# Attention on one core: projection units reordered, the 128-column score blocks put last, weights turned in score banks, the last half's sums taken on TensorE

## Chip, cores, metric

One core of a Trainium2 chip (trn2), float32 throughout. The metric is the device time of one execution in microseconds (us). Executions of one kernel agree within 0.2%. The experiments were made in four sessions on four chips, each time with the kernel before beside them (medians 1990.3 to 1991.0), so a few tenths of a microsecond between sessions mean nothing. What is read from a trace comes from one profiled execution of each kernel. Engines: PE is TensorE, PEld its weight loads, ACT ScalarE, DVE VectorE, POOL GpSimd, SP the engine that issues most DMAs. A line number such as L255 is a line of the kernel that the profile belongs to, so the numbers shift between kernels.

## What is computed

Batch 32, 256 channels, 1024 positions, 8 heads of 32. Cut to what matters:

```python
def reference(x, q_w, q_b, kv_w, kv_b):
    xn = group_norm(x, groups=32)                      # no scale, no shift
    q = einsum('oc,bcs->bos', q_w, xn) + q_b           # per head: 32 x 1024
    k, v = split(einsum('oc,bcs->bos', kv_w, xn) + kv_b)
    s = q.T @ k / sqrt(32)                             # strictly lower triangle, else -10000
    a = softmax(where(mask == 0, -10000, s)); a = where(mask == 0, 0, a)
    return x + (a @ v.T).T
```

## The kernel before

The score work of one batch is cut into 12 visits. I number them 0 to 11. A visit makes scores for four heads against one key block of 512 columns ("full") and one of 256 ("half"), runs three exponentials on ACT (heads 0 and 1, heads 2 and 3, the half), one projection unit on PE with its eviction on ACT, and then the products with V of the visit before. Scores have six PSUM banks. Projections and key sums (the sums of the exponentials over the keys) share **one** bank (`misc`). In the profile lines sT are scores, pp and ppv projection units (of q or k, and of V), acc the products with V, pd the key sums and den their copy. In visits 1, 5, 7 and 11 the full block of each head is two pieces, of 384 and of 128 columns.

```python
def projections(b):
    qk = [[q unit, k unit] for g in range(2) for hf in range(2)]   # (shortened)
    v = [lambda n=n: project_v(b, n) for n in range(4)]
    return qk[0] + v[:1] + qk[1] + v[1:3] + qk[2] + v[3:] + qk[3]
...
def piece(g, hf, k, part=None):
    d = k - hf * BPH
    if d == 1:                                        # two blocks: 384 and 128 columns
        blocks = [(k, slice(P, HALF), slice(P, HALF)), (k + 2, slice(0, P), slice(3 * P, HALF))]
    ...
def scores(b, full, half):
    ...
    first = [scores_of((b, half), short[:, j % 2, 1, :], j, name) for j in (2, 3)]
    for j in range(4):
        scores_of((b, full), pairs[j // 2][:, j % 2, :], j, name)     # all blocks of a head
    for ins in first:
        ins.then_inc(bank_free, 1)
    wait = nc.tensor.wait_ge(bank_free, live["free"])                 # "the gate"
    for j in range(2):
        lo = scores_of((b, half), short[:, j, 0, :], j, name)         # late products
    for a in range(2):
        nc.scalar.activation(e[:, 2 * a : 2 * a + 2, :], pairs[a], AF.Exp)
    exp = nc.scalar.activation(eh..., short, AF.Exp)
    mask(full, e); mask(half, eh)                                     # on GpSimd
...
for i in range(B * N + 1):                 # the order on every engine is the program's
    scores(i // N, *visits[i % N])
    for f in at.pop(i, ()): f()            # a projection unit with its eviction
    values((i - 1) // N, ...)              # products with V, DVE adds exponentials up
    for f in after.pop(i, ()): f()         # key sums (pd), norm statistics (pm, pv), finishes
...
# last batch: rows of sums of three halves fetched at N-2, inverted and broadcast at N-1
```

## Time and profile before

| | before |
|---|---|
| median of 3 runs | 1991.79 us (1989.82 to 1992.19) |
| span of the profiled run | 1990.4 us |
| first scores / start of the second batch (visit 12) | 22.77 / 88.68 us |
| one steady batch, score start to score start | 60.61 us |
| last batch's start / last score group's start / end | 1907.12 / 1958.62 / 1990.4 us |

I read the kernel as three parts: a start up to the second batch, thirty equal batches, and the last batch with the end. A hundredth of a microsecond in one visit of every batch is 0.3 us of the time. The visit lengths below are means over the steady batches, from the starts of the first score product of each visit. The profile lines of before stand in the prediction.

### The profile page before, as it was taken

To read this page: it belongs to the slowest core of one execution; us is meant where nothing else is said; L and a number is where in the kernel's file an instruction comes from. 1 tells how busy PE (TensorE), PEld (TensorE's weight loads), DVE (VectorE), ACT (ScalarE), POOL (GpSimd) and SP (SyncE) were. 2 spreads that over 40 slices of the span, in tenths; PEclk is the share of its full clock that TensorE was granted. 3 is DMA by queue.
4 is the path that set the end of the run, shared out by engine and by line. 5 is a ranking of instruction groups with operands and counts; after the bars stand their busy time and mean duration, and the time that the engine had idled before them with its cause. 6 is when DMAs were issued, how large, how long until landed. Compare 5 with 4: busy or idle time off the path is not lost.

```text
span 1990.4 us, 54612 instructions
## 1 busy us (share of the span) xinstructions
PE 1941.6 (98%) x24078; PEld 961.9 (48%) x24078; DVE 1559.4 (78%) x1608; ACT 1462.8 (73%) x1863; POOL 580.1 (29%) x495
## 2 busy tenths in 40 slices
PE   6999999999999999999999999999999999999995
PEld 3444544444544445545444454454444454544442
DVE  3787878877878877878878788778788787887777
ACT  4777777777777777777777777777777777777773
POOL 1323323323223323233233233232232332332321
PEclk9999999999999999999999999999999999999997
DMA  2011111111111111111111111111111111111011
GB/s 104 2 67 41 51 47 65 66 51 47 54 52 66 67 41 51 52 61 66 59 43 52 49 66 67 41 51 55 57 66 67 35 54 49 66 66 45 31 35 68
DMA packets 56800, 108.04 MB, mean 54 GB/s; under 512 B 14189, under 2 KB 15341, under 8 KB 56557
## 3 DMA queue, kind: packets, MB, share of 16 engines
q1 hardware_dynamic: 54780, 103.56, 14.7%
q8 instruction: 191, 3.13, 0.7%
q10 hardware_dynamic: 1776, 0.92, 0.2%
q14 instruction: 53, 0.43, 0.1%
HBM read 68.82 MB, written 35.64 MB: 52 GB/s over the span
## 4 chain that ended last, share of the span: by engine, by line
PE 91%; ACT 5%; issue 2%; DVE 1%; DMA 1%; ACTq 0%; POOL 0%; SPq 0%; DVEq 0%
PE sT L255 29%; PE pp L147 24%; PE acc L325 23%; PE ppv L147 9%; PE pd L343 6%; ACT e L302 3%; ACT v L225 1%; ACT eh L303 1%; DMA rb<-inverses 0%; DVE e L330 0%; DMA qk_bias<-in_L_conv_q_b_dram 0%; PE pm L147 0%; PE pv L147 0%; DVE rb L389 0%; DVE rb L388 0%
## 5 line engine op out<-in xcount | busy, mean ns | idle before, releaser
L302 ACT ACTIVATE e<-sT 128x1024 f32<-128x1024 f32 x768 | 744.9, 1022 | 278.5 <-PE sT L255 232.4
L330 DVE TENSOR_TENSOR e<-e,eh 128x1024 f32<-128x1024 f32 x384 | 543.8, 1430 | 384.0 <-PE acc L325 363.4
L270 POOL TENSOR_SCALAR_AFFINE_SELECT e<-e 128x512 f32<-128x512 f32 (+1 forms) x256 | 390.7, 1526 | 1360.9 <-ACT e L302 1185.4
L330 DVE TENSOR_TENSOR e<-e,e 128x1536 f32<-128x1536 f32 (+2 forms) x384 | 638.2, 1662 | 17.3 <-POOL e L270 2.0
L255 PE MATMUL sT<-q,k 32*128 32x256 f32 (+3 forms) x7168 | 618.1, 460 | 0.8 <-ACT k L209 0.8
L255 PEld LDWEIGHTS sT<-q,k 32*128 32x128 f32 x7168 | 463.3, 184 | 203.6 <-issue 106.7
L147 PE MATMUL pp<-xn,wT 128*32 128x512 f32 x4096 | 495.9, 602 | 2.4 <-DVE xn L192 0.9
L325 PE MATMUL acc<-e,v 128*32 128x512 f32 (+2 forms) x4096 | 400.7, 486 | 0.9 <-POOL e L270 0.9
L303 ACT ACTIVATE eh<-sT 128x1024 f32<-128x1024 f32 x384 | 396.0, 1031 | 0.0
L147 PE MATMUL ppv<-wT,xn 128*32 128x256 f32 x4096 | 247.6, 382 | 1.3 <-ACT k L209 1.3
L325 PEld LDWEIGHTS acc<-e,v 128*32 128x32 f32 x4096 | 132.6, 110 | 224.9 <-issue 200.4
L325 PE MATMUL acc<-eh,v 128*32 128x256 f32 x3072 | 225.1, 380 | 9.5 <-ACT v L225 9.5
L147 PEld LDWEIGHTS pp<-xn,wT 128*32 128x32 f32 x4096 | 107.3, 109 | 230.2 <-issue 216.6
L348 ACT COPY den<-pd 128x512 f32<-128x512 f32 x128 | 75.0, 586 | 187.7 <-PE pd L343 187.7
L325 PEld LDWEIGHTS acc<-eh,v 128*32 128x32 f32 x3072 | 96.2, 110 | 182.6 <-issue 134.0
L147 PEld LDWEIGHTS ppv<-wT,xn 128*32 128x32 f32 x4096 | 120.0, 109 | 96.8 <-issue 20.6
L270 POOL TENSOR_SCALAR_AFFINE_SELECT eh<-eh 128x512 f32<-128x512 f32 x128 | 164.1, 1282 | 2.6
L343 PE MATMUL pd<-e,pick 128*32 128x512 f32 x1024 | 135.7, 599 | 7.1 <-DVE e L330 7.1
L389 DVE SCALAR_TENSOR_TENSOR rb<-rb,v_bias_col,x 128x512 f32<-128x512 f32 x129 | 96.5, 748 | 4.6
L209 ACT ACTIVATE q<-pp,qk_bias 128x512 f32<-128x512 f32 x128 | 89.8, 702 | 6.3 <-PE pp L147 6.3
L209 ACT ACTIVATE k<-pp,qk_bias 128x512 f32<-128x512 f32 x128 | 89.8, 702 | 3.8 <-PE pp L147 3.8
L388 DVE TENSOR_TENSOR rb<-num,rb 128x512 f32<-128x512 f32 x129 | 87.7, 680 | 1.6 <-DMA rb<-inverses 1.5
(45 smaller groups left out, 497.7 us busy)
## 6 DMA issues: line engine op xcount, KB each, us to landing
x<-in_x_dram SPq DMA_DIRECT2D x64, 512.0 KB
rb<-inverses SPq DMA_DIRECT2D x127, 256.0 KB
out_dram<-rb SPq DMA_DIRECT2D x127, 256.0 KB
sums<-den SPq DMA_DIRECT2D x128, 8.0 KB
rows<-sums SPq DMA_DIRECT2D x31, 32.0 KB
inverses<-inv SPq DMA_DIRECT2D x31, 32.0 KB
wn<-in_L_conv_kv_w_dram ACTq DMA_DIRECT2D x2, 256.0 KB
wn<-in_L_conv_q_w_dram ACTq DMA_DIRECT2D x1, 256.0 KB
```

Source lines behind the costliest of these rows:

```text
L147: nc.tensor.matmul(out[part], lhsT=lhsT[:, part], rhs=rhs, start=start, stop=stop, skip_group_check=True)
L209: nc.scalar.activation(live[key][:, cols], pp, AF.Identity, bias=qk_bias[:, n, g : g + 1], scale=(SCALE, 1.0)[n],)
L255: ins = nc.tensor.matmul(pair[:, cols], lhsT=live["k", b, g][rows, kb * P : (kb + 1) * P], rhs=live["q", b, g][rows, hf * HALF + of.start ...
L270: nc.gpsimd.affine_select(out=diagonal, in_=diagonal, pattern=[[0, 4], [0, n], [1, P]], compare_op=ALU.is_gt, fill=0.0, base=0, channel_mu ...
L302: nc.scalar.activation(e[:, 2 * a : 2 * a + 2, :], pairs[a], AF.Exp)
L303: exp = nc.scalar.activation(eh.rearrange("p (n bank) q -> p bank n q", n=2), short, AF.Exp)
L325: nc.tensor.matmul(acc[HD * j : HD * (j + 1), of], lhsT=live["v", b][:, kb, h * HD : (h + 1) * HD], rhs=e[:, j, cols], start=first, stop=l ...
L330: nc.vector.tensor_add(total[:, :, of], total[:, :, of], e[:, :, cols])
L343: nc.tensor.matmul(pd[HD * j : HD * (j + 1), :], lhsT=pick, rhs=total[:, j, :], start=True, stop=True, skip_group_check=True,)
L348: nc.scalar.copy(den, pd)
L388: nc.vector.tensor_mul(rb[:, g, cols], num[:, g, cols], rb[:, g, cols])
L389: nc.vector.scalar_tensor_tensor(rb[:, g, cols], rb[:, g, cols], v_bias_col[:, g : g + 1], xt[:, g, cols], ALU.add, ALU.add)
```

## The change

Its intent, part by part: take away a wait for V in visit 1 by making V earlier; put the 128-column blocks after everything else so that they fill the score group better; start the weights in idle score banks and keep PE's clock up with filler products; take the last half's sums on PE instead of adding on DVE, and split the last batch's inversion so that part of it runs early.

```diff
-            return qk[0] + v[:1] + qk[1] + v[1:3] + qk[2] + v[3:] + qk[3]
+            return qk[0] + v[:2] + qk[1] + v[2:] + qk[2] + qk[3]
@@ scores
             for j in range(4):
-                scores_of((b, full), pairs[j // 2][:, j % 2, :], j, name)
+                scores_of((b, full), pairs[j // 2][:, j % 2, :], j, 0)      # 384 (or all) columns
             (gate and late products as before)
-            for a in range(2):
-                nc.scalar.activation(e[:, 2 * a : 2 * a + 2, :], pairs[a], AF.Exp)
-            exp = nc.scalar.activation(eh..., short, AF.Exp)
+            two = len(full[4]) == 2
+            if two:
+                for j in range(4):
+                    scores_of((b, full), pairs[j // 2][:, j % 2, :], j, 1)  # 128 columns
+            for a in (2, 0, 1) if two else (0, 1, 2):                       # 2 is the half bank
+                (the same exponentials)
@@ start: weights turned in score banks, fillers, first projections in two banks
+            load_weights(); turn_weights(0); norm_channels...; keep_busy(4)
+            norm_mean(0); turn_weights(1); norm_deviation(0); norm_variance(0); norm_rstd(0)
+            turn_weights(2); keep_busy(6)
@@ last batch
+                        for i in (N - 1, N):      # the last pieces summed on PE, into one bank
+                            when(first + i, lambda b=b, i=i: sum_pieces(b, products[i - 1], i == N - 1, i == N), after)
-                    when(first + N - 2, lambda b=b: gather(b, every[:3]))
-                    (check and invert three halves at N - 1)
+                    for v, ns in ((N - 4, every[:2]), (N - 2, every[2:3])):
+                        when(first + v, lambda b=b, ns=ns: gather(b, ns))
+                        when(first + v + 1, lambda b=b, ns=ns: check_sums(b, ns))
+                        when(first + v + 1, lambda b=b, ns=ns: invert(b, ns))
```

Not in the cut: the first projections take turns in two banks, the scaling of the biases goes from GpSimd to DVE, and the final check and count of the sums go ahead of the last two finishes. The rest of the diff moves code and gives helpers a name.

## The prediction

> **What bounds the kernel now.** I read the page first, then the waits of the steady part, then the timeline of single visits, then both ends.
>
> ```profile
> PE 1941.6 (98%) x24078; PEld 961.9 (48%) x24078; DVE 1559.4 (78%) x1608; ACT 1462.8 (73%) x1863; POOL 580.1 (29%) x495
> ...
> PE 91%; ACT 5%; issue 2%; DVE 1%; DMA 1%; ACTq 0%; POOL 0%; SPq 0%; DVEq 0%
> ```
>
> TensorE (PE) holds the path nearly everywhere. A batch is 12 visits; I number them 0 to 11. On PE a visit is: scores (sT), one projection unit (pp or ppv), the value products of the visit before (acc), sometimes key sums (pd). Score starts in the trace put a batch at 60.6 us in the whole steady part, each visit the same to within some ns. So a change per visit is paid 31 or 32 times. In the steady part the table of waits holds two lines that matter:
>
> ```profile
> PEld pd L343 <- ACT k L209: 10.5, 29, 0.4
> ...
> PE acc L325 <- ACT v L225: 8.6, 29, 0.3
> ```
>
> The second is one wait per batch, in visit 1, for a V eviction. The timeline of PE in visit 1, and of PE and ScalarE (ACT) in visit 7, which has the same work without that wait:
>
> ```profile
> 1002.73 1.67 PE L255 MATMUL sT<-q,k 32*128 32x256 f32 x24
> 1004.33 1.93 PE L147 MATMUL ppv<-wT,xn 128*32 128x256 f32 x32
> 1006.08 1.04 PE L325 MATMUL acc<-e,v 128*32 128x512 f32 x8
> 1007.42 0.64 PE L325 MATMUL acc<-eh,v 128*32 128x256 f32 x8 [0.30 <-ACT v L225]
> 1007.85 1.07 PE L343 MATMUL pd<-e,pick 128*32 128x512 f32 x8
> ```
>
> ```profile
> 1033.46 1.67 PE L255 MATMUL sT<-q,k 32*128 32x256 f32 x24
> 1035.06 1.92 PE L147 MATMUL pp<-xn,wT 128*32 128x512 f32 x16
> 1036.80 1.04 PE L325 MATMUL acc<-e,v 128*32 128x512 f32 x8
> 1037.66 0.61 PE L325 MATMUL acc<-eh,v 128*32 128x256 f32 x8
> 1038.15 1.06 PE L343 MATMUL pd<-e,pick 128*32 128x512 f32 x8
> ```
>
> ```profile
> 1034.67 1.94 ACT L302 ACTIVATE e<-sT 128x1024 f32<-128x1024 f32 x2 [0.52 <-PE sT L255]
> 1036.50 1.03 ACT L303 ACTIVATE eh<-sT 128x1024 f32<-128x1024 f32 x1
> 1037.40 0.70 ACT L209 ACTIVATE k<-pp,qk_bias 128x512 f32<-128x512 f32 x1
> ```
>
> Read start to start: from the acc start to the pd start is 1.77 us in visit 1 and 1.35 in visit 7, so the V wait costs 0.42 us a batch. But see visit 7: the k eviction ends at 1038.10 and pd starts at 1038.15. There is one bank for projections and sums, ACT does the three exponentials before the eviction, and pd waits for it. PE has **no slack left** against ACT there: what delays the exponentials delays pd.
>
> At the two ends:
>
> ```profile
> 13.82 3.64 PE L147 MATMUL pp<-xn,wT 128*32 128x512 f32 x16 [0.86 <-DVE xn L192]
> 18.32 3.64 PE L147 MATMUL pp<-xn,wT 128*32 128x512 f32 x16 [0.86 <-ACT q L209]
> 22.77 1.57 PE L255 MATMUL sT<-q,k 32*128 32x256 f32 x16 [0.81 <-ACT k L209]
> ```
>
> ```profile
> 1971.90 1.93 PE L343 MATMUL pd<-e,pick 128*32 128x512 f32 x8 [7.07 <-DVE e L330]
> ```
>
> The first projections take 3.64 us where steady ones are 1.75 apart, and at the end PE waits 7 us for VectorE (DVE) sums.
>
> **What the Trainium skill says.** (1) "TensorE: Matmul & The Clock Gate", Part 1, "What's actually happening": the clock is halved until PE has been busy for a window of about 3.4 us. Agrees: the 3.64 us above are twice the later ones, and the granted clock first reads full at 22.0 us, after unbroken work from 18.3. (2) Same page, Part 3, "The mechanism": a weight load is pulled ahead of running products only for another row group. The four heads of a score group are four row groups; the trace shows each row's next load start as its previous product starts, so order within a row matters. (3) "Perfetto Trace Analysis", "Matmuls": independent groups should rotate through PSUM banks, so evictions overlap. The pd wait of visit 7 is what one bank costs. (4) Same page, "Tensor Engine Instruction": ACT and DVE are strict first-in first-out, and ends of products are estimates; so I measure start to start on PE, and take ACT's order as fixed.
>
> **V units moved.** The order of units goes from qk v qk v v qk v qk to qk v v qk v v qk qk, a qk being two units. V1 is now done two visits before its use: the wait of visit 1 goes, 0.42 us. In exchange the rest slides one visit later. q of the second half is now made in visit 0 and used by the first scores of visit 1; k of the second group is made in visit 5 and used by the first scores of visit 6. In visit 0 the eviction ends 4.62 us after the visit's start and PE wants it at 4.65: with a 0.05 lag that costs 0.02. Visit 5 is worked out below, since it also has the second change.
>
> **128-column blocks last.** Four visits (1, 5, 7, 11) have them. Their score group lasts 1.60 us to the next start, against 1.50 in the others (1008.85 to 1010.35): 0.10 is to be won. But the two late 256-column products wait on a semaphore for the first two to end. In an ordinary visit that gate opens 0.79 us in:
>
> ```profile
> 1009.64 0.19 PEld L255 LDWEIGHTS sT<-q,k 32*128 32x128 f32 x2
> ```
>
> A row that holds only 384 columns before the gate is idle from about 0.75; with a fresh load (0.11) it streams again at 0.90. Then 256 columns (0.43) and 128 (0.21) end at 1.54, and the next group starts 0.09 later: 1.63. So I expect **no gain, some 0.03 loss**: the small blocks had filled that gap.
>
> The larger effect is on ACT. In these visits the exponential of the half bank now goes first, and its products lie behind the gate: 0.79, plus 0.70 from a fresh load to the end of two such products (first pair of a group), plus 0.05 for the semaphore: the first exponential starts at 1.54. Before it was 1.21 (1034.67 less 1033.46). The eviction ends 3.43 after that start (1038.10 less 1034.67), pd or a dependent score starts 0.05 later: 1.54 + 3.48 = 5.02 us into the visit.
> - Visit 7: pd at 5.02 instead of 4.69 (1038.15 less 1033.46): +0.33.
> - Visit 1: now a k unit; pd at 5.02 instead of 5.12: -0.10 is all that remains of the 0.42.
> - Visit 5: now a k unit that the next scores need: length 5.02 instead of 4.76: +0.26.
> - Visit 11: a V unit, nobody waits: +0.03. Visit 0: +0.02.
> Sum: +0.54 a batch. Times 31, and about 0.6 for the first batch, which has no pd in visit 1: **+17 us**.
>
> **The start.** Weights are turned in score banks, so no pool stands in the way; the bias scaling leaves GpSimd's queue, where it held the averaging matrix back until 10.3 us; the group statistics can go once the fillers end. Four fillers of 256 columns at half clock are some 0.85 each: 6.1 to 9.5 at most. From that product to the first projection took 3.47 (10.35 to 13.82); the six further fillers (0.43 warm, 0.85 cold) end about 1 us after that. So projections start near 14.2, but warm: 2 x 1.75, then 0.85 for the last eviction, and no wait between them since the second has its own bank. First scores at 18.5 instead of 22.77: -4.3. Visit 0 lasted 10.3 us with three units waiting for one bank; I get 1.50 + 3 x 1.75 + 0.8 for an eviction + 0.2 = 7.75: -2.5. Visit 1 gives 0.5. Together **-7**.
>
> **The end.** The last half's sums leave DVE: its additions ran from 1964.4 to 1971.9. PE instead sums pieces while it waits for masks, and adds 1.3 us after the last values: pd complete near 1967.7, against 1973.8. Then one eviction (0.6), two reciprocals of 1.75, one finish (1.5), the check of the sums, whose two small transfers now lie beside the reciprocals, and 1.8 for the last finish: DVE ends near 1976.5 instead of 1984.7. The three 256 KB transfers that landed at 1976.4 become one. The branch at the end is not shortened (5.7 us). **-8**, with 1 or 2 either way.
>
> Sum: 1991.8 + 17 - 7 - 8 = 1994. Changes of this kind are mostly kept because they paid, so I shade to **1992**.
>
> **Rivals.** (a) The author's sum: the V wait gone (0.42) and 0.10 in four visits, 0.82 x 31 = 25 us, and 15 at the ends: 1952. For it: both terms are visible in the trace. Against it: pd at 1038.15 sits on an eviction at 1038.10, and the exponentials can't start before the gate. (b) The blocks do give the 0.10 because the gate opens earlier than in ordinary visits, and the exponentials start near 1.40: visits 1, 5, 7 then give -0.24, +0.13, +0.19, visit 11 -0.10, so the steady part is even and the time 1977. (c) ACT is late as I say, and DVE or GpSimd masks, which start later too (after the third exponential), come too late for the value products of visits 6 and 0: I get some 0.1 to 0.4 us of room; if it is gone, up to 0.3 more in two visits, 2010.
>
> **Range and chances.** My mechanism about 0.75, (b) or something between it and (a) 0.2, (c) 0.05. The ends are uncertain by 3 us, the steady sum by 4. Range 1978 to 2001. More than 2% faster means under 1952, only (a) in full: 0.03. Slower than 2032: 0.005.
>
> **What would show it.** In the profile after: batches of 61.1 us between score starts (60.6 before; under 60.3 and I am wrong); no wait of acc for v; pd in visits 1 and 7 about 5.0 us after the score start with a k eviction ending just before; the first scores of visit 6 waiting for a k eviction; the first exponential of the four visits 1.5 us in; their score group at 1.60 or more to the next start; first scores near 18.5; the last DVE instruction 8 us nearer to the last values. If pd in visit 7 starts at 4.7, the ACT step is wrong and the time is near 1970.

## The result, and the profile after

The changed kernel took **2000.82 us** (median of 4 runs, 2000.64 to 2001.10) against 1991.81 for the kernel before on the same chip. The ratio is 1.0047, interval [1.0030, 1.0065]: within 2%, but clearly slower. Ratios here are the mean time of one kernel's runs over that of the other's of the same rounds, so not quite the ratio of the medians.

| part, from the two traces | before | after | difference | predicted |
|---|---|---|---|---|
| start to visit 12 | 88.68 | 81.80 | -6.9 | -6.4 |
| 30 steady batches | 30 x 60.61 | 30 x 61.25 | +19.1 | +16.2 |
| last batch and end | 83.28 | 79.65 | -3.6 | -7.5 |
| span | 1990.4 | 1999.0 | +8.6 | +2.3 |

The "predicted" column sorts the prediction's own terms: -7 and the first batch's +0.6; 30 times 0.54; -8 and the last batch's 0.54.

The steady visits, in us:

| visit | 0 | 1 | 4 | 5 | 7 | 11 | batch |
|---|---|---|---|---|---|---|---|
| before | 4.652 | 6.117 | 4.837 | 4.754 | 5.691 | 4.744 | 60.61 |
| after | 4.670 | 6.019 | 4.894 | 5.024 | 6.019 | 4.801 | 61.25 |

First the page of the changed kernel, the two lines that answer to those of before:

```profile
PE 1957.1 (98%) x24138; PEld 957.4 (48%) x24138; DVE 1588.5 (79%) x1607; ACT 1461.6 (73%) x1860; POOL 546.2 (27%) x494
...
PE 64%; ACT 13%; issue 10%; DVE 8%; POOL 2%; DMA 2%; SPq 0%; ACTq 0%; DVEq 0%; POOLq 0%
```

PE is still busy 98%, yet its share of the chain fell from 91% to 64% and ACT's rose from 5% to 13%: busy time hides it, the chain shows it. Then the waits of the steady part (what waited for what: us in total, times, longest):

```profile
PEld pd L358 <- ACT k L221: 37.3, 58, 0.6
...
PEld sT L267 <- ACT k L221: 18.7, 29, 0.6
```

Before, the first of these was 10.5 us and 29 times. The line of V products waiting for a V eviction (8.6 us before) is gone. So the wait that the change aimed at was removed, and another took its place. The timeline of visit 7 shows which, PE first and then ACT:

```profile
1036.42 1.72 PE L267 MATMUL sT<-q,k 32*128 32x256 f32 x24
1038.07 1.92 PE L159 MATMUL pp<-xn,wT 128*32 128x512 f32 x16
...
1041.44 1.06 PE L358 MATMUL pd<-e,pick 128*32 128x512 f32 x8 [0.16 <-ACT k L221]
```

```profile
1037.96 1.02 ACT L320 ACTIVATE eh<-sT 128x1024 f32<-128x1024 f32 x1 [0.85 <-PE sT L267]
1038.88 1.94 ACT L322 ACTIVATE e<-sT 128x1024 f32<-128x1024 f32 x2
1040.69 0.70 ACT L221 ACTIVATE k<-pp,qk_bias 128x512 f32<-128x512 f32 x1
```

ACT's first exponential starts 1.54 us into the visit (1037.96 less 1036.42; before 1.21). The four ACT instructions then run without a gap, the eviction ends at 1041.39, and pd starts at 1041.44, 5.02 into the visit (before 4.69). The score group itself lasts 1.65 (1038.07 less 1036.42; before 1.60). In visit 5 the same eviction holds the next visit's scores:

```profile
1031.58 0.71 PE L267 MATMUL sT<-q,k 32*128 32x256 f32 x4 [0.16 <-ACT k L221]
```

The visit started at 1026.56, so it lasted 5.02. The bracketed 0.16 is only the idle time directly ahead of the product; weight loads and the modelled ends hide the rest, which is why start to start is the measure.

At the start (PE):

```profile
13.76 3.64 PE L159 MATMUL pp<-xn,wT 128*32 128x512 f32 x32
18.21 1.57 PE L267 MATMUL sT<-q,k 32*128 32x256 f32 x16 [0.81 <-ACT k L221]
```

Two units in 3.64 us, where before one took that; first scores at 18.21 instead of 22.77. At the end (DVE):

```profile
1975.24 1.23 DVE L349 TENSOR_TENSOR e<-e,eh 128x1024 f32<-128x1024 f32 x1
1980.60 0.22 DVE L401 SCALAR_TENSOR_TENSOR in_range<-rows,in_range 32x64 f32<-32x64 f32 x1 [4.13 <-DMA rows<-sums]
...
1984.53 3.36 DVE L435 RECIPROCAL rb<-pd 128x256 f32<-128x256 f32 x2
1989.41 0.69 DVE L423 TENSOR_TENSOR rb<-num,rb 128x512 f32<-128x512 f32 x1 [1.52 <-DMA rb<-inverses]
```

DVE stood 4.13 us in front of the check of the third half's sums, and behind that check were the finishes and the last reciprocals. PE had the last half's sums complete at 1981.46, 3.1 us before those reciprocals began. SP's queue tells why the rows came so late:

```profile
1970.77 1.16 SPq L414 DMA_DIRECT2D rb<-inverses  x2
1971.98 0.51 SPq L386 DMA_DIRECT2D sums<-den  x1
...
1979.01 0.34 SPq L396 DMA_DIRECT2D rows<-sums  x1
```

The 8 KB of sums were issued at 1971.98, just behind two broadcasts of 256 KB each, and had landed only by 1979.0, when the fetch could go. The chain that ended last (followed back through the profile of the changed kernel) runs through this transfer (6.96 us), and later through that of the **last** half's sums: 5.13 us from 1985.09, behind the third half's broadcast of 256 KB, issued at 1983.67. DVE waited 0.67 us for the rows of that one, so the two chains end close together.

### The profile page after: what moved, and what is told of

Read it like the earlier page. It is cut to its first block, busy times and chain, and to the rows that moved or that the text cites. A ratio compares the mean times of both kernels' runs of the same rounds, so it can differ in the third digit from the quotient of the medians.

```text
span 1999.0 us, 54756 instructions
## 1 busy us (share of the span) xinstructions
PE 1957.1 (98%) x24138; PEld 957.4 (48%) x24138; DVE 1588.5 (79%) x1607; ACT 1461.6 (73%) x1860; POOL 546.2 (27%) x494
## 4 chain that ended last, share of the span: by engine, by line
PE 64%; ACT 13%; issue 10%; DVE 8%; POOL 2%; DMA 2%; SPq 0%; ACTq 0%; DVEq 0%; POOLq 0%
PE sT L267 22%; PE acc L344 14%; PE pp L159 12%; PE ppv L159 9%; DVE e L349 7%; ACT e L322 7%; PE pd L358 6%; ACT eh L320 4%; ACT k L221 3%; POOL e L282 2%; DMA sums<-den 1%; DMA wn<-in_L_conv_kv_w_dram 0%; PE pm L159 0%; DMA x<-in_x_dram 0%; PE pv L159 0%
## 5 line engine op out<-in xcount | busy, mean ns | idle before, releaser
L349 DVE TENSOR_TENSOR e<-e,eh 128x1024 f32<-128x1024 f32 x382 | 551.8, 1458 | 334.1 <-PE acc L344 313.9
L282 POOL TENSOR_SCALAR_AFFINE_SELECT e<-e 128x512 f32<-128x512 f32 (+1 forms) x256 | 386.4, 1509 | 1414.4 <-ACT e L322 1146.0
L349 DVE TENSOR_TENSOR e<-e,e 128x1536 f32<-128x1536 f32 x381 | 635.2, 1667 | 44.8 <-POOL e L282 33.5
L267 PEld LDWEIGHTS sT<-q,k 32*128 32x128 f32 x7168 | 454.5, 184 | 225.5 <-issue 107.0
L358 PE MATMUL pd<-e,pick 128*32 128x512 f32 (+1 forms) x1048 | 136.7, 595 | 11.6 <-ACT k L221 10.2
L282 POOL TENSOR_SCALAR_AFFINE_SELECT eh<-eh 128x512 f32<-128x512 f32 x128 | 107.4, 839 | 0.1
```

The lines of the kernel that those rows point to most:

```text
L267: ins = nc.tensor.matmul(pair[:, cols], lhsT=live["k", b, g][rows, kb * P : (kb + 1) * P], rhs=live["q", b, g][rows, hf * HALF + of.start ...
L282: nc.gpsimd.affine_select(out=diagonal, in_=diagonal, pattern=[[0, 4], [0, n], [1, P]], compare_op=ALU.is_gt, fill=0.0, base=0, channel_mu ...
L349: nc.vector.tensor_add(total[:, :, of], total[:, :, of], e[:, :, cols])
L358: nc.tensor.matmul(pd[HD * j : HD * (j + 1), of], lhsT=pick, rhs=e[:, j, cols], start=start, stop=stop, skip_group_check=True,)
```

## The experiments

Theory **A**: the steady loss is ACT's. The half bank's exponential goes first and has to wait for the late products; the eviction comes behind three exponentials; pd (visits 1, 7) and the next scores (visit 5) wait for the eviction. Rivals: the score group of PE itself got longer; V's new place costs; the masks come late. Theory **T** for the end: the third half's small transfers, not the last half's sums. "End" in the table is from the start of the last score group to the end of the span; among the thirteen it is 26.6 to 28.3 wherever the tail works as in the changed kernel.

| run | ratio to before | median, us | batch, us | end, us |
|---|---|---|---|---|
| before | 1 | 1991.8 | 60.61 | 31.8 |
| after | 1.0047 | 2000.82 | 61.25 | 27.62 |
| r1_blocks_back | 0.9885 [0.9869, 0.9902] | 1968.06 | 60.21 | 27.22 |
| r2_units_back | 1.0079 [1.0063, 1.0096] | 2006.78 | 61.42 | 27.96 |
| r3_both_back | 0.9947 [0.9931, 0.9964] | 1980.45 | 60.61 | 27.09 |
| r4_before_gate | 0.9970 [0.9953, 0.9987] | 1984.96 | 60.78 | 26.89 |
| r5_evict_early | 0.9895 [0.9879, 0.9912] | 1970.63 | 60.28 | 27.82 |
| r6_by_pairs | 0.9857 [0.9841, 0.9874] | 1962.83 | 60.07 | 26.58 |
| r7_no_fill | 1.0050 [1.0033, 1.0067] | 2001.09 | 61.25 | 27.39 |
| r8_tail_queue | 1.0040 [1.0023, 1.0057] | 1999.49 | 61.26 | 25.77 |
| r9_tail_order | 1.0056 [1.0039, 1.0072] | 2001.21 | 61.26 | 27.27 |
| r10_best_a | 0.9808 [0.9792, 0.9824] | 1952.33 | 59.69 | 28.27 |
| r11_best_b | 0.9786 [0.9769, 0.9802] | 1947.61 | 59.50 | 27.69 |
| r12_tail_direct | 1.0031 [1.0014, 1.0048] | 1997.47 | 61.26 | 24.07 |
| r13_best_c | 0.9765 [0.9749, 0.9781] | 1944.54 | 59.50 | 25.15 |

All were correct.

### 1. Each steady part taken back by itself

Blocks and exponentials as before (r1), with V moved and the new ends:

```diff
-                scores_of((b, full), pairs[j // 2][:, j % 2, :], j, 0)
+                scores_of((b, full), pairs[j // 2][:, j % 2, :], j)
-            if two: (the 128-column blocks after the gate)
-            for a in (2, 0, 1) if two else (0, 1, 2):
+            for a in (0, 1, 2):
```

> The changed kernel with the score order inside a visit as before: each head's 128 columns right after its 384, exponentials of the two pairs first. V units stay moved, both ends stay changed. Theory A (the late exponential delays the eviction that PE waits for): the first exponential is back at 1.21 us into visits 1 and 7, so pd starts at 4.69 in both; visit 1 is 5.69, visit 7 is 5.69, visit 5 is 4.76, visit 11 is 4.75; a batch is 60.25 us between score starts (61.25 in the changed kernel), and the time is about 1969. Rival B (the block order costs only its 0.05 us of PE in four visits, and the moved units cost the rest): a batch is 61.05, visits 5 and 7 stay near 5.0 and 6.0, the time is about 1994.

Units as before from the second batch on (r2), with the blocks last:

```diff
+            if b:
+                return qk[0] + v[:1] + qk[1] + v[1:3] + qk[2] + v[3:] + qk[3]
             return qk[0] + v[:2] + qk[1] + v[2:] + qk[2] + qk[3]
```

> The changed kernel with the V units of batches 1 to 31 where they were; 128-column blocks stay last, ends stay changed. Theory A: visit 1 holds a V unit whose eviction ends near 4.87, so the second value products start at 4.92 and pd at 5.35: visit 1 is 6.35; visit 7 stays 6.02; visit 5 is 4.80, since nothing waits for a V eviction there; a batch is about 61.3 us, the same as the changed kernel, time 2000 to 2003: with blocks last, moving the V units is worth nothing. Rival B (moved units are what costs): a batch near 60.8, time about 1987.

Both of these edits together (r3), which leaves only the new ends:

> Only the two ends changed; the steady part as in the kernel before. Every theory: a batch of 60.61 us, and the start and the end worth what the traces show, 7.5 and about 4 us: 1980. If the time is over 1984, the ends are worth less than I read from the traces.

Measured: r1 1968.06 with visits 1, 5, 7, 11 at 5.691, 4.744, 5.690, 4.754; r2 2006.78 with visit 1 at 6.448 (I had expected 6.35), visit 5 at 4.800, visit 7 at 6.019; r3 1980.45. The expectation of r2 missed: with the blocks last I had thought the moved units worth nothing and the time 2000 to 2003. ACT in visit 7 of r1, which starts at 1019.83 and lasts 5.69:

```profile
1021.04 1.94 ACT L318 ACTIVATE e<-sT 128x1024 f32<-128x1024 f32 x2 [0.52 <-PE sT L267]
1022.86 1.03 ACT L316 ACTIVATE eh<-sT 128x1024 f32<-128x1024 f32 x1
1023.76 0.70 ACT L221 ACTIVATE k<-pp,qk_bias 128x512 f32<-128x512 f32 x1
```

First exponential at 1.21, as in the kernel before. What follows: against r3, moving the units alone gives 0.40 us a batch (60.61 to 60.21), as large as the V wait was. Putting the blocks last alone costs 0.81 (60.61 to 61.42). Together they cost 0.64: with the blocks last the moved units still give 0.17 (61.42 to 61.25), and not 0.40, because they put into visit 5 a k that the next scores need, exactly where the eviction became late (visit 5 is 4.800 in r2, 5.024 in the changed kernel). The ends are worth 10.5 us (r3).

### 2. The eviction put ahead of the third exponential

In visits 1, 5 and 7 only ACT's order changes: half bank, heads 0 and 1, eviction, heads 2 and 3; GpSimd masks the half first.

```diff
-                (exponential of heads 2, 3 and both masks inside scores())
+                late = scores(i // N, *visits[i % N], early=i % N in (1, 5, 7))
                 for f in at.pop(i, ()):      # the unit and its eviction
                     f()
+                for f in late:               # exponential of heads 2, 3, then its mask
+                    f()
```

> The changed kernel, with nothing altered on PE: in visits 1, 5 and 7 alone ScalarE evicts the projection before its third exponential instead of after it (and GpSimd masks the half bank first). Theory A (PE waits for an eviction that stands behind three exponentials): the eviction runs from about 3.6 to 4.3 us, PE waits for nothing there, and pd starts at its own pace, 4.68 us into visits 1 and 7, whose length falls from 6.02 to 5.68; visit 5 falls from 5.02 to 4.79. A batch is 60.35 us, the time about 1972. Rival B (PE's order of products is what costs): nothing moves, 2001. Rival D (ScalarE has no room, so the late third exponential takes back the gain through the score banks or the masks): visits 2, 6 and 8 grow by up to 0.3 each, 1980 to 1990.

Measured: 1970.63; visits 1 and 7 at 5.649, visit 5 at 4.791; PE's program is that of the changed kernel, and its score group still lasts 1.64 (1022.71 less 1021.07). PE and ACT in visit 7, which starts at 1021.07:

```profile
1021.07 1.72 PE L267 MATMUL sT<-q,k 32*128 32x256 f32 x24
1022.71 1.92 PE L159 MATMUL pp<-xn,wT 128*32 128x512 f32 x16
...
1025.75 1.04 PE L366 MATMUL pd<-e,pick 128*32 128x512 f32 x8
```

```profile
1022.61 1.02 ACT L321 ACTIVATE eh<-sT 128x1024 f32<-128x1024 f32 x1 [0.79 <-PE sT L267]
1023.53 1.02 ACT L325 ACTIVATE e<-sT 128x1024 f32<-128x1024 f32 x1
1024.71 0.69 ACT L221 ACTIVATE k<-pp,qk_bias 128x512 f32<-128x512 f32 x1 [0.16 <-PE pp L159]
```

The first exponential is as late as in the changed kernel (1.54), but the eviction ends 4.33 into the visit instead of 4.97, pd starts at 4.68 instead of 5.02, and the visit is 0.37 shorter. So it is not PE's group that costs, and not the late exponential as such: it is **the eviction in line behind it**. This is what shows theory A. Visit 6's score group grew by 0.06, but the visit did not (4.839; 4.836 in the changed kernel), so the late third exponential cost no time that can be seen.

### 3. The blocks ahead of the gate, in two orders

A cheaper way to use ACT's time would be small blocks that don't delay the exponentials. First (r4) all 384-column blocks, then all 128-column blocks, then the gate, exponentials as before:

```diff
             for j in range(4):
                 scores_of((b, full), pairs[j // 2][:, j % 2, :], j, 0)
+            if len(full[4]) == 2:
+                for j in range(4):
+                    scores_of((b, full), pairs[j // 2][:, j % 2, :], j, 1)
             (gate, late products; no blocks after them; exponentials 0, 1, 2)
```

> V units moved, ends changed, the 128-column blocks of all four heads after all 384-column ones but before the gate, exponentials of the two pairs first. Theory A: no row idles at the gate and no load comes late, so the score group of visits 1, 5, 7, 11 takes 1.50 us to the next start (1.60 before, 1.65 changed); the first exponential starts near 1.18, pd at 4.66 in visits 1 and 7 (their length 5.66), visit 5 is 4.74, visit 11 is 4.65: a batch of 60.1, time about 1964. Rival C (128-column products cost extra wherever they stand, since a weight load takes longer than they do): the group stays at 1.60 and a batch at 60.25, as in the run with the blocks put back.

This missed: 1984.96 instead of 1964. The score group became 1.51 as expected, but the first exponential started at 1.42, not 1.18. ACT in visit 7 of r4, which starts at 1028.77:

```profile
1030.19 1.94 ACT L321 ACTIVATE e<-sT 128x1024 f32<-128x1024 f32 x2 [0.73 <-PE sT L267]
```

In the records of single products, the blocks of heads 0 and 1 that this exponential reads had ended 1.15 into the visit. The 384-column blocks of heads 2 and 3, which it doesn't read but which stand ahead of the 128-column blocks in the program, ended at 1.34. (The records don't name the head; I tell them apart by size and order.) So I put up theory **A2**: a wait for PE is met when everything up to the awaited product in program order is done. That the exponential waited for a later product instead is ruled out if the modelled ends are right: the next products of the visit that raise the semaphore which ACT waits for ended at 1.57 and 1.58, after it had started. The next kernel (r6) keeps pairs of heads together, heads 0 and 1 first:

```diff
-            for j in range(4):
-                scores_of((b, full), pairs[j // 2][:, j % 2, :], j, 0)
+            for a in range(2):
+                for n in range(len(full[4])):
+                    for j in (2 * a, 2 * a + 1):
+                        scores_of((b, full), pairs[a][:, j % 2, :], j, n)
```

> V units moved, ends changed; in the four visits the order is heads 0 and 1: 384 columns, then their 128; then heads 2 and 3 likewise; then the gate and the late products; exponentials of the pairs first. In the run with all 384-column products first, the first exponential started at 1.43 though its own products ended at 1.14: it started 0.08 after products of heads 2 and 3 that stand before them in the program (end 1.35). Theory A2 (a wait for PE counts all products up to that place in the program): with the pairs kept together the first exponential starts at 1.20, the group takes 1.51, visits 1 and 7 are 5.68, visit 5 is 4.74, visit 11 is 4.66, a batch 60.1, the time about 1965. Rival (the exponential was late for another reason, a bank written by the other heads): it stays at 1.43 and the time at 1985.

Measured: 1962.83; visits 1 and 7 at 5.673, 5 at 4.729, 11 at 4.667; group 1.51. ACT in visit 7, which starts at 1017.47:

```profile
1018.66 1.94 ACT L320 ACTIVATE e<-sT 128x1024 f32<-128x1024 f32 x2 [0.50 <-PE sT L267]
1020.49 1.03 ACT L318 ACTIVATE eh<-sT 128x1024 f32<-128x1024 f32 x1
1021.39 0.70 ACT L221 ACTIVATE k<-pp,qk_bias 128x512 f32<-128x512 f32 x1
```

The first exponential is at 1.19. What makes the pair a clean test: in the two kernels every one of the 24 score records of visit 7 starts within 0.01 us of the same offset. PE did the same at the same times; only the program order, and with it what the exponential waited for, differs, and the exponential moved by 0.23 us.

### 4. The start without fillers

```diff
-            keep_busy(4)
-            keep_busy(6)
```

> The changed kernel without its ten filler products at the start. If the fillers are worth the whole start gain, the first scores fall back from 18.2 to 22.7 us, and the time to 2005. My reading: without them the group statistics go 1 us earlier and the first projections follow at once, cold (3.64 us each, no wait between them) until a window of work has passed; first scores between 18.0 and 20.0, time 2000.5 to 2002.5.

Measured: 2001.09, first scores at 18.50:

```profile
11.93 5.77 PE L159 MATMUL pp<-xn,wT 128*32 128x512 f32 x32 [1.03 <-DVE xn L204]
18.50 1.57 PE L267 MATMUL sT<-q,k 32*128 32x256 f32 x16 [0.81 <-ACT k L221]
```

Without fillers the first two units take 5.77 us instead of 3.64, but start 1.83 earlier (11.93 against 13.76), since the group averages no longer stand behind fillers. First scores in the other runs lie between 17.9 and 18.8, so the fillers are worth nothing that can be measured. The gain of the start must be in the rest, which no run shows part by part: no pool and no GpSimd work ahead of the averaging matrix, a second bank for the first projections, and a shorter first visit (10.28 to 7.76).

### 5. The end

First (r8) the last batch's broadcasts were issued from GpSimd's queue, out of the way of the small transfers:

```diff
-                nc.sync.dma_start(out=live["rb", b][...], in_=live["inv", b][n]...broadcast_to(...))
+                (nc.gpsimd if b == B - 1 else nc.sync).dma_start(...)
```

> The changed kernel; in the last batch alone the broadcasts of the inverses leave from GpSimd's queue, so the small transfers of the sums do not stand behind them on SyncE's. Theory T (the third half's 8 KB transfer, issued at 1971.98, ended only at 1979.0 because 512 KB of broadcasts were ahead of it on the same queue, and VectorE waited 4.1 us for it in order): it lands in about 2 us, the wait goes, and from the last score start to the end takes about 23.5 us instead of 27.6; the time is about 1997. Rival (the 16 engines are full, whatever the queue): the transfer still takes 5 us or more, the end is within 1 us of 27.6, the time 2000 to 2001.

Measured: end 25.77, a gain of 1.85 where 4 was expected, and 0.8 below the least of the others. DVE's wait went from 4.13 to 2.58:

```profile
1980.24 0.22 DVE L401 SCALAR_TENSOR_TENSOR in_range<-rows,in_range 32x64 f32<-32x64 f32 x1 [2.58 <-DMA rows<-sums]
```

The fetch of the rows was issued at 1973.78 instead of 1979.01, but the rows still took until about 1980.2: they landed 0.2 us after the second of the broadcasts (1980.01). So the queue is a part of it, the company of other transfers another: the 512 KB of broadcasts, and a store of 256 KB that SP had issued at 1973.39, just ahead of the fetch; r8 doesn't tell these two apart. The last half's 8 KB gained more: issued at 1985.06 while the third broadcast was under way on GpSimd's queue (1982.81 to 1988.81), they took 1.70 us instead of 5.13. The edit also had a side effect: GpSimd issued the broadcasts from 1972.21 on and so came late with its masks, and PE's products with V waited for them:

```profile
1976.63 1.94 PE L344 MATMUL acc<-e,v 128*32 128x512 f32 x8 [2.09 <-POOL e L282]
```

The last half's sums were complete 12.1 us after the last score group's start instead of 10.1. The end didn't hang on that, since DVE stood 0.40 us for the third half's broadcast behind the reciprocals. Second (r9), the broadcasts were to be issued after the fetch:

```diff
-            for n in ns: (broadcasts inside invert)
+            if not (b == B - 1 and ns.start == 0):
+                spread(b, ns)
+                    when(first + N - 2, lambda b=b: spread(b, every[:2]))   # after the gather of half 3
```

> The changed kernel, with one edit in the last batch: the two broadcasts of inverses for the first channel group are issued after the sums of the third half have been fetched back, so the two small transfers no longer stand behind 512 KB. Theory T (the end lost what I expected because the small transfers stood behind the broadcasts, and DVE, in order, waited 4.1 us for them): the rows of the third half land near 1976, DVE's wait of 4.1 us for them goes, and last score to end falls from 27.6 to 24 to 25.5 us. Rival (the end is set by the chain through the last sums and two reciprocals, the wait is only slack in it): 27 or more. Steady part unchanged, time 1997 to 1999 under T.

This **tested nothing**. Only PE, ACT, DVE and GpSimd keep the program's order in this kernel; SP's queue is ordered by the scheduler, which put the broadcasts first again:

```profile
1971.24 1.16 SPq L418 DMA_DIRECT2D rb<-inverses  x2
1972.44 0.51 SPq L386 DMA_DIRECT2D sums<-den  x1
```

Third (r12), no transfer at all ahead of the reciprocals: DVE inverts the third half's sums straight from their bank, and its rows are fetched later with the last half's, for the check alone.

```diff
+        def invert_third(b):
+            for c in range(2):
+                within = slice(c * HALFBANK, (c + 1) * HALFBANK)
+                nc.vector.reciprocal(live["rb", b][:, NG - 1, within], live["pd", b, 2][:, within])
-                    for v, ns in ((N - 4, every[:2]), (N - 2, every[2:3])):
+                    for v, ns in ((N - 4, every[:2]),):
+                    when(first + N, lambda b=b: invert_third(b))
-                    for n in every[:2]: (finish)
+                    for n in every[:3]: (finish)
-            check_sums(B - 1, every[3:])
+            check_sums(B - 1, every[2:])
```

(The last half's sums move to a score bank, so that the two don't share one.)

> The changed kernel with one edit in the last batch: VectorE takes the inverses of the third half from its sums in the bank (two reciprocals of 1.7 us) instead of from rows that two small transfers bring and a broadcast brings back; the rows are fetched with the last half's for the check alone, and the last half's sums use a score bank. Theory T (the small transfers stood between the additions and the reciprocals): no wait of 4.1 us for rows; additions end near 1976.5, third half's reciprocals to 1980, finishes to 1984.5, last reciprocals to 1988, check and last finish to 1991: last score to end 23.5 to 24.5 instead of 27.6. Rival (the end hangs on the last half's own sums on PE and the check of them): 26.5 or more. Steady part unchanged; time 1996 to 1998 under T.

Measured: end 24.07, 3.5 less than the changed kernel, as expected. DVE:

```profile
1976.00 1.23 DVE L349 TENSOR_TENSOR e<-e,eh 128x1024 f32<-128x1024 f32 x1
1977.14 3.36 DVE L442 RECIPROCAL rb<-pd 128x256 f32<-128x256 f32 x2
...
1984.91 3.36 DVE L435 RECIPROCAL rb<-pd 128x256 f32<-128x256 f32 x2
1989.06 0.22 DVE L401 SCALAR_TENSOR_TENSOR in_range<-rows,in_range 64x64 f32<-64x64 f32 x1 [0.79 <-DMA rows<-sums]
```

DVE no longer waits between additions and reciprocals; it pays 3.36 us of extra reciprocals and still ends earlier, because the third half's finish no longer waits for a broadcast that comes back at 1989.4. From the last score group's start to DVE's last instruction it takes 19.8 us here, 23.3 in the changed kernel, 26.0 before. Theory T is shown as far as the third half's round trip goes (two small transfers, check, broadcast), which r12 takes off the path as a whole. Its rival, that PE completes the last half's sums too late, falls: they were complete 10.1 us after the last score group's start in the changed kernel and 10.2 in r12. One thing changed along with it: the transfer of the last half's sums took 1.70 us (from 1985.40) instead of 5.13, now that no broadcast stood ahead of it, and what that alone is worth is not shown.

### 6. A faster version

The order by pairs, with early evictions too, the pairs' first exponential leading: in visits 1, 5 and 7 (r10), and in visits 0, 4 and 6 as well (r11).

```diff
+                late = scores(i // N, *visits[i % N], early=i % N in (1, 5, 7))             # r10
+                late = scores(i // N, *visits[i % N], early=i % N in (0, 1, 4, 5, 6, 7))    # r11
+            for a in (0, 2, 1) if early else (0, 1, 2):   # heads 0,1; half; eviction; heads 2,3
```

> Pairs of heads kept together (as in the run by pairs), and in visits 1, 5 and 7 the exponential of heads 0, 1 first, then the half bank, then the projection's eviction, then the exponential of heads 2, 3; last batch as in the run before. Theory A2 (what is left of the loss in visits 1, 5 and 7 is the eviction behind three exponentials): visits 1 and 7 near 5.55, visit 5 near 4.65, batch 59.75, time 1950 to 1954. Rival (with the eviction early, masks or score banks become the bound, as visit 6's score group of 1.56 hinted): batch 59.95 or more, time 1957 or more.

> As the run before, with the early eviction in visits 0 and 4 and 6 too. Theory: visits 0 and 4 were 4.67 and 4.89 in the changed kernel, because their evictions end late; early they lose up to 0.15 each, batch 59.6, time 1946 to 1950. Rival (masks late, score banks freed late): batch no shorter than in the run before.

Measured: r10 1952.33, visits 1 and 7 at 5.515, visit 5 at 4.657, batch 59.69; visit 6's score group is 1.56, as the rival had it, but the visit is no longer for it (4.841; 4.836 in r6). r11 1947.61, batch 59.50: visit 4 went from 4.838 to 4.681 and visit 6 from 4.841 to 4.743, and visits 1, 5 and 7 gave up to 0.05 of it back. Both kernels still carry r9's edit, which does nothing. With r12's end instead (r13):

> The fastest steady part so far (pairs of heads together, early evictions in visits 0, 1, 4, 5, 6, 7: 1947.6 us, batch 59.50) with the end of the run before. If the two add: 1944 to 1946, batch 59.50. If the end is set by something else once visits are shorter: 1947 or more.

Measured: 1944.54, ratio 0.9765: the gains add (1947.61 less 1944.54 is 3.1), and the kernel beats the one before by 2.35%.

## Why the prediction was right or wrong, point by point

**Right: what bounds the kernel and which wait replaces which.** The first exponential was predicted at 1.54 and came at 1.54; pd and the end of visit 5 at 5.02 and came at 5.02; the V wait went; scores of visit 6 wait for k. Visits 0, 1, 5 and 7 came within 0.01 us of the predicted lengths. Experiments 1 and 2 show the cause as the prediction gave it. Rival (a) saw both terms of the gain rightly, since r1 gets the V wait's 0.40 and r6 a part of what the group gives (60.21 to 60.07 a batch), but not that this order of the blocks forfeits them. Rival (b) needed exponentials at 1.40 and a shorter group; neither came. Rival (c), late masks, was not needed for any of it.

**A little off: the size of the steady term, +0.54 against +0.64.** Visit 4 is missing from the sum. It grew by 0.057: its exponentials start at 1.25 instead of 1.19, so its eviction ends later, and the group averages wait for the bank. r11, which lets that eviction go first, takes 0.16 off visit 4, so it too was bound by ACT, which I had not looked at. The packed trace shows where the 0.06 comes from: in the changed kernel ACT has one more semaphore instruction there (an instruction that only waits; the views leave these out), at 1.19, where the exponential otherwise starts, and the exponential follows at 1.25. It is there in every steady visit 4 of the seven kernels whose visit 4 starts its exponentials at 1.25 (the changed one, r2, r5, r7, r8, r9, r12) and in none of the eight that start them at 1.19; PE's score products in that visit are at the same offsets. So it comes with the blocks put last, whether the units are moved or not. Of the rest, 0.03 is in visit 11: the group is 1.65, not 1.63. Over thirty batches this is 2.9 us.

**Right in size, in part by luck: the start**, -6.9 against -6.4: the first scores came 4.6 earlier (4.3 predicted), visit 0 was 2.5 shorter, as predicted. But the part I gave to the warm clock was wrong: I reckoned projections "near 14.2, but warm", and they were, yet without fillers the same scores come at 18.50 instead of 18.21.

**Wrong: the end.** This is the largest miss: of the 6.3 us by which the sum of the terms fell short (2.3 against 8.6), 3.9 are here, 2.9 in the steady part, and the start gave 0.5 back. The prediction said -8; the changed kernel gained 4.2 there from the last score group on (31.8 to 27.6; the 3.6 of the table has the last batch's longer visits in it). The step that failed is the list that follows "pd complete": "one eviction (0.6), two reciprocals of 1.75, one finish (1.5), the check of the sums, whose two small transfers now lie beside the reciprocals". It has no term for the **third** half, whose sums now go out alone, behind the two broadcasts that the same change had moved early; they took 7 us to land, and DVE, which takes its work in order, stood 4.13 us with the reciprocals behind it. Then, with the reciprocals done, it waited 1.52 more for the broadcast that comes of them: so the third half's round trip held the end here, and not the late reciprocals. The last half's sums were mis-sized too: pd was complete 10.1 us after the last score group's start, where the prediction had 9.1 (1967.7 less 1958.62), and their own transfer, not sized at all, took 5.13 us and ended on the path as well. I had counted it a gain that "The three 256 KB transfers that landed at 1976.4 become one". r12 takes these transfers off the path, and the end is 7.7 us shorter than before. The -8 agrees with that only in sum: the last instruction of DVE came 6.3 nearer to the last scores in r12, and 1.4 came from the stretch behind it (5.7 before, 4.3 after), which I had said would not be shortened. The change put the count of bad sums ahead of the last two finishes, so DVE had it 1.7 us before its last instruction ended; no run shows that this is the reason.

**A reading too strict, without effect.** The trace doesn't bear out the "only" of point (2): in visit 7 of the kernel before, loads start at 0.32 and 0.44 us together with products of what the order makes the same rows, and run 0.185 us beside them. No term of the sum rests on it.

**Wrong: the shading.** The sum of the terms was 1994, and I lowered it to 1992 because such changes are mostly kept. That put the number on top of the time before, where the working itself said slower. The terms as measured (-6.9, +19.1, -3.6) give +8.6, the difference of the spans.

## What to carry to other kernels

When ACT stands close behind PE, ask of a new order on PE which ACT instruction will wait for its last product, and what is queued behind that one: here 0.3 us at the first exponential came out unreduced at an eviction three instructions later. In r4 against r6, ACT's wait for PE was met only once the products ahead of the awaited one in the program had ended as well; so try keeping the products that one reader needs next to each other. For a tail, write down every small transfer with what is issued just ahead of it and what stands behind it on the engine that reads it; taking a value from the bank where it already lies was cheaper here, at 3.4 us of work, than a round trip beside 512 KB.

## What the Trainium skill lacked or had wrong

- "TensorE: Matmul & The Clock Gate", Part 3, "The mechanism", has matmuls start and end strictly in program order. In r4 the 128-column blocks of heads 0 and 1 are recorded as ended 1.15 us into the visit, the 384-column blocks of heads 2 and 3, ahead of them in the program, at 1.34 (ends are modelled; the second records of the latter also start later, at 0.86 against 0.76). The section concludes that one signal on the last product is sound; it does not say what that costs a reader of earlier products: with products at the same times the exponential started at 1.42 (r4) or at 1.19 (r6), by program order alone.
- "DMA: Bandwidth & Descriptors", "Issuing engines are not separate DMA queues", says that transfers from different issuing engines run on the same DMA engines and interleave. r8 agrees as far as it goes: from another queue than the broadcasts, the rows still took 6.4 us beside them (and behind a store of 256 KB on their own queue). Not in the section is what a small transfer pays: here 8 KB took about 7 us on the same queue behind 512 KB, 5.1 us behind 256 KB, and 1.7 us where that broadcast was on another queue (r8) or not there (r12).
- No page has what a warm clock is worth in a start that waits for other things too: ten fillers of 256 columns changed the first two units from 5.77 to 3.64 us, and the first scores by 0.3 us, within the spread of 17.9 to 18.8 among the runs.
- No page has the case of one in-order ACT that does exponentials and evictions: moving one exponential behind one eviction in three visits of twelve was worth 30 us of 2000 (r5 against the changed kernel).
- The pages give no cost for a wait that takes a semaphore instruction of its own on ACT: in visit 4 the exponential started 0.06 us later with it (1.25 against 1.19), 1.7 us over thirty batches.
